# Two attention layers on one core: layer 1's sums of weights travel through DRAM instead of TensorE, and two kinds of steps change places

## The chip, the core and the metric

The kernel runs on one NeuronCore of a Trainium2 chip. Its engines run side by side and meet only through semaphores: TensorE (PE in the profile; PEld is its weight load), VectorE (DVE), ScalarE (ACT), GpSimd (POOL) and SyncE (SP), which here only issues DMAs. Each engine works off its own instructions in order. The metric is the device time of one execution in microseconds (us): 4741.2 us before the change, the median of three runs from 4740.61 to 4742.43.

## The reference, cut to what matters

The input has 2 images of 256 channels and 64 x 64 pixels, so 4096 positions each. Layer 0 is an attention over four heads of 16 channels with a gate; the change doesn't touch it. Layer 1, which the change is about, is this:

```python
qkv = jnp.einsum('oc,bchw->bohw', w_qkv, x) + b_qkv[None, :, None, None]
qkv = qkv.reshape(b, HEADS, 3 * head_dim, h * w)          # 4 heads of 64
q, k, v = jnp.split(qkv, 3, axis=2)
attn = jax.nn.softmax(jnp.einsum('bhdn,bhdm->bhnm', q, k) * scale, axis=-1)
out = jnp.einsum('bhnm,bhdm->bhnd', attn, v).reshape(b, c, h, w)
return jnp.einsum('oc,bchw->bohw', w_out, out) + b_out[None, :, None, None] + x
```

Note the reshape: the attention's output has the positions ahead of the head's channels, so it is read as channels only after it went through DRAM (the arrays `att`). Everything is float32.

## The kernel before, in words

**Tiling of layer 1.** A unit is `(b, g, j)`: one image, one pair of heads, one block of 512 queries; there are 32 units, worked off one after the other. A unit's 4096 keys come in 32 chunks of 128. A *step* of the loop at the end of the function handles two chunks, so a unit has 16 steps, and I count the steps of a unit from 0. The partitions of a score tile are 128 keys; its 1024 columns are 512 queries for each of the two heads.

**Work of one chunk.** PE multiplies keys with queries (`score`, L861). DVE takes the running maximum over the chunks (`keep`, L878), then ACT copies the scores to a tile `raw` in SBUF (L879). Ten steps later (`LAG`) DVE subtracts the maximum (`shift`, L944), ACT takes the exponential (`weigh`, L956), POOL adds the weights to an accumulator (L966 for the first two chunks of a group, L968 for all others), and PE multiplies the weights with the values (`gather`, L978). The tiles `raw` are a ring of 24.

**Groups.** A unit's chunks form two groups of 16. After the last chunk of each group the maximum is turned by PE (L886), folded by DVE (L898), split by POOL into three bfloat16 parts (`split`, L909 to L912), and turned back by PE (`turn`, L925): for group 0 in steps 8 and 9 of the unit, for group 1 in steps 0 and 1 of the next. ACT copies the row (L930), PE spreads it (L939), and only then can `shift` begin on that group. Because of the lag, the weights of group 0 are made from step 10 on, those of group 1 from step 2 of the next unit on. When a group's values are complete, ACT copies the result out of PSUM into a tile `avs` (L995), of which the pool has two buffers: for group 0 in step 2 of the next unit, for group 1 in its step 10.

**End of a unit,** in steps of the next unit: `total` (step 12) sums the accumulators over the 128 keys by PE into rows; `keep_total` copies them to SBUF (L1016); `turn_total` (step 13) turns the rows by four PE transposes (L1023), so that each query is on its own partition; `factors` joins both groups' sums and takes the reciprocal on DVE (L1035, L1036, L1038), and POOL makes the factor for group 0 (L1039). `turn_sums` turns each group's result (L1023), and `rows` multiplies it with the factor on DVE (L1049); POOL adds a bias (L1056) and joins the groups (L1060). In step 13 this is done for group 1, in step 14 for group 0. Then the rows go to `att` in DRAM.

**Work ahead.** The queries of the next unit are made in steps 14 and 15 (`next_queries`, L672; copied by ACT, L699). While units remain that have no keys and values yet (the first 24 units), each unit makes one block of them in steps 4 to 7. The output of image 0 is projected in four of the later units (`project_out`). One PSUM bank, `misc`, serves all of these small products in turn.

**What sets the order.** `at(t, place, step)` hangs a function onto a step at a named place: "start" and "early" come after the two score products, "early end" after the first chunk's `keep` and `shift`, "late" and "late end" after the second chunk's `keep` and after `gather`. Compute instructions keep this written order on every engine; DMAs are placed by the scheduler and wait, in order, on their queue. At the end `FILL` spreads first halves of the last output's projection over what is left.

Of the kernel before, what the change touches and what calls it, by code (L numbers as in the profile page):

```python
# [8 lines left out]
F32 = mybir.dt.float32  # L9
BF16 = mybir.dt.bfloat16  # L10
AF = mybir.ActivationFunctionType
ALU = mybir.AluOpType
# [3 lines left out]
P = 128  # L16
NB = 512
# [4 lines left out]
D1 = 64  # L22
# [5 lines left out]
def conv_attention_kernel(  # L28
# [739 lines left out]

    units = [(b, g, j) for b in range(B) for g in range(PR) for j in range(NJ)]
# [8 lines left out]
    with (  # L778
# [22 lines left out]
        )  # L801
        last_att = []
# [210 lines left out]
        def keep_total(u):  # L1013
            b, g, j = u
            row = l1.tile([P, NB], F32, tag="srow", bufs=1, name=f"srow_{b}_{g}_{j}")
            seq(nc.scalar.copy(row, srows[u]))  # L1016
            srows[u] = row
            seq(nc.scalar.activation(losts[u], losts[u], AF.Exp, scale=D1**-0.5))

        def turned(a, name):  # L1020
            ps = misc(name)
            for i in range(PB):
                seq(nc.tensor.transpose(ps[:, bass.ts(i, P)], a[:, bass.ts(i, P)], ident))  # L1023
            return ps.rearrange("p (i k d) -> p i k d", k=2, d=D1)

        def turn_total(u):
            srows[u] = turned(srows[u], "sumt_{}_{}_{}".format(*u))

        def factors(u):

            b, g, j = u
            ps = srows.pop(u)
            lost = losts.pop(u).rearrange("p k i -> p i k")
# [11 lines left out]
        def rows(u, n):  # L1045
            b, g, j = u
            ps = avs1.pop((u, n))
            r = l1.tile([P, PB, 2, D1], F32, tag="rows", name=f"rows_{b}_{g}_{j}_{n}")
            seq(nc.vector.tensor_tensor(  # L1049
                r, ps, joined[u][:, n].unsqueeze(3).to_broadcast([P, PB, 2, D1]), ALU.mult  # L1050
            ))
            last = u == units[-1]
            if n == 1:
                halves[u] = r
                bias = b1v[:, 2 * g : 2 * g + 2, :].unsqueeze(1).to_broadcast([P, PB, 2, D1])
# [53 lines left out]
        for n, u in enumerate(units):  # L1109
            b, g, j = u  # L1110
            t0 = n * US
            if n > 0:
                at(t0 - 5, "start", lambda u=u, b=b, j=j: fetch(("q", u), x1[b][j]))
                at(t0 - 2, "late", lambda u=u: next_queries(u, 0))
                at(t0 - 1, "early", lambda u=u: next_queries(u, 1))
                at(t0 - 1, "early end", lambda u=u: keep_queries(u))
# [24 lines left out]
            at(t1 + 5, "early", lambda u=u: turn_total(u))  # L1141
            at(t1 + 5, "early end", lambda u=u: factors(u))
            at(t1 + 5, "late", lambda u=u: turn_sums(u, 1))
            at(t1 + 5, "late end", lambda u=u: rows(u, 1))
            at(t1 + 6, "early", lambda u=u: turn_sums(u, 0))
            at(t1 + 6, "early end", lambda u=u: rows(u, 0))
            if b < B - 1 and (g, j) == (PR - 1, NJ - 1):
                for i in range(NJ):
                    t1 = t0 + US + (i + 4) * GS // 2
                    at(t1, "start", lambda b=b, i=i: fetch_output(b, i))  # L1150
                    for o in range(CC):
                        at(
                            t1 + 3 + 4 * o, ("early", "late")[o],
                            lambda b=b, i=i, o=o: project_out(b, i, o, misc(f"o1_{b}_{i}_{o}")),
                        )
                        at(t1 + 3 + 4 * o, "late end", lambda b=b, i=i, o=o: output(b, i, o))
# [51 lines left out]
        for i in range(NJ - 2):  # L1208
# [7 lines left out]
            (END + GS // 2 + 4, "early end"): (3,), (END + GS // 2 + 5, "early end"): (4,),  # L1216
            (END + GS // 2 + 5, "late end"): (5,), (END + GS // 2 + 6, "early end"): (6, 7),
# [87 lines left out]
```

## Time and profile before

| what | value |
|---|---|
| median of three runs | 4741.2 us |
| the profiled execution | 4741.58 us, of which 4739.8 us are the profile's span |
| layer 1's loop | about 2060 us to 4700 us of the span |
| one unit that makes keys and values | 81.30 us from its first L879 to the next unit's |
| one unit that makes none (the last 8) | 79.19 us |
| one of the four units with output | 88.75 us (the first of them 90.01 us) |
| PE, DVE, ACT, POOL busy in 2692.30 to 2773.60 us, one unit of 81.30 us | 76.70, 76.34, 68.51, 75.48 us |

The profile is of one execution; it gives, for every engine, the start and duration of each instruction and, where an engine was idle before it, whose semaphore ended the idle time. A row of a timeline has the start in us, the duration in us, engine, line and operation, output and inputs, and in brackets the idle time before it with its releaser. A row of the table of stages has a stretch and then the busy time of each engine in it. "SPq" is SyncE's DMA queue: the row tells when a DMA was issued, not when its data had landed.

### The profile page before, as it was taken

Reading aid. Unit: us, or ns where it says so; the run is one execution under the profiler, and the core shown is the slowest. Engines: PE = TensorE matmul, PEld = TensorE weight load, DVE = VectorE, ACT = ScalarE, POOL = GpSimd, SP = SyncE. Lnnn points to the kernel's source line nnn. Section 1 sums busy time; section 2 is a strip of 40 time slices with the busy share of each in tenths; the row PEclk is TensorE's granted clock in tenths of the full one; section 3 lists DMA queues with packets and bytes.
Section 4 is the critical chain, followed back from the end, with each engine's and each line's share of the span. In section 5 each row is a group of like instructions: output and inputs, shape, how many; then the busy total and the mean of one; then the engine's idle time right before and its main releaser. Section 6 shows DMA issues by size and latency. Waiting matters only on the chain.

```text
span 4739.8 us, 70643 instructions
## 1 busy us (share of the span) xinstructions
PE 4526.9 (96%) x27506; PEld 1496.2 (32%) x27506; DVE 3917.0 (83%) x4584; ACT 3394.1 (72%) x4508; POOL 2540.6 (54%) x1491
## 2 busy tenths in 40 slices
PE   8999999999999999989999999999999999999998
PEld 3433333333333333333232232323233332222222
DVE  6777777777777777359999999999999899999996
ACT  3366666666666666668888888888887778888884
POOL 6300000000000000039999999999998889999994
PEclk9999999999999999999999999999999999999999
DMA  3100000000000000110000100001111111000002
GB/s 103 34 4 19 19 21 15 15 15 15 15 15 15 15 13 13 57 63 25 23 25 17 54 30 23 25 23 36 52 36 45 63 52 47 18 14 7 14 16 74
DMA packets 113381, 140.10 MB, mean 30 GB/s; under 512 B 51864, under 2 KB 52696, under 8 KB 112932
## 3 DMA queue, kind: packets, MB, share of 16 engines
q1 hardware_dynamic: 111260, 135.11, 9.2%
q8 instruction: 216, 3.54, 0.3%
q14 instruction: 121, 0.99, 0.1%
q10 hardware_dynamic: 1784, 0.46, 0.0%
HBM read 93.58 MB, written 41.70 MB: 29 GB/s over the span
## 4 chain that ended last, share of the span: by engine, by line
PE 58%; DVE 15%; POOL 15%; issue 6%; ACT 5%; DMA 1%; SPq 0%; ACTq 0%; DVEq 0%; POOLq 0%
PE s L448 24%; POOL acc L968 13%; PE av L463 12%; DVE rmax L878 10%; PE s L861 6%; PE av L978 5%; DVE raw L944 4%; ACT raw L879 4%; PE a L410 2%; PE p L270 1%; PE k1p L672 1%; POOL acc L966 1%; PE rt L886 1%; PE q1p L672 1%; PE o L549 1%
## 5 line engine op out<-in xcount | busy, mean ns | idle before, releaser
L968 POOL TENSOR_TENSOR acc<-acc,raw 128x1024 f32<-128x1024 f32 x884 | 2098.1, 2373 | 89.4 <-ACT raw L956 30.2
L414 DVE TENSOR_REDUCE mx<-a 128x1 f32<-128x512 f32 x2048 | 1315.3, 686 | 450.5 <-PE a L410 449.4
L451 ACT ACTIVATE p<-s 128x512 f32<-128x512 f32 x2048 | 1109.8, 597 | 701.3 <-PE a L410 367.3
L944 DVE TENSOR_TENSOR raw<-raw,shift 128x1024 f32<-128x1024 f32 x1024 | 1238.0, 1213 | 19.2 <-PE shift L939 12.7
L861 PE MATMUL s<-q,k 64*128 64x512 f32 x4096 | 1117.2, 636 | 142.9 <-ACT raw L879 134.6
L878 DVE TENSOR_TENSOR rmax<-s,rmax 128x1024 f32<-128x1024 f32 x960 | 1170.1, 1219 | 72.7 <-PE s L861 70.8
L879 ACT COPY raw<-s 128x1024 f32<-128x1024 f32 x1024 | 1037.7, 1013 | 259.4 <-DVE rmax L878 173.5
L448 PE MATMUL s<-q,kT 32*128 32x512 f32 x4096 | 1219.1, 640 | 0.0
L956 ACT ACTIVATE raw<-raw 128x1024 f32<-128x1024 f32 x1024 | 1086.9, 1062 | 178.4 <-DVE raw L944 147.3
L410 PE MATMUL a<-kT,q 32*128 32x512 f32 x4096 | 1129.7, 643 | 1.2 <-DVE mx L414 1.0
L978 PE MATMUL av<-raw,v 128*64 128x512 f32 x4096 | 999.3, 606 | 2.0
L463 PE MATMUL av<-p,v 128*32 128x256 f32 (+1 forms) x7904 | 650.2, 399 | 0.6 <-ACT avs L477 0.6
L861 PEld LDWEIGHTS s<-q,k 64*128 64x128 f32 x4096 | 317.1, 185 | 827.9 <-ACT raw L879 628.0
L513 POOL TENSOR_TENSOR f<-f,dyn 128x16 f32<-128x16 f32 x15 | 3.3, 223 | 1028.2 <-DVE f L512 1028.2
L448 PEld LDWEIGHTS s<-q,kT 32*128 32x128 f32 x4096 | 397.9, 183 | 426.3 <-issue 392.1
L978 PEld LDWEIGHTS av<-raw,v 128*64 128x64 f32 x4096 | 243.3, 136 | 587.6 <-issue 428.8
L463 PEld LDWEIGHTS av<-p,v 128*32 128x32 f32 x7904 | 157.6, 108 | 751.5 <-issue 737.3
L564 POOL TENSOR_SCALAR res<-res 128x1024 f32<-128x1024 f32 x16 | 16.8, 1049 | 660.5 <-ACT res L563 660.5
L410 PEld LDWEIGHTS a<-kT,q 32*128 32x128 f32 x4096 | 305.0, 184 | 31.4 <-DVE mx L414 18.2
L966 POOL TENSOR_TENSOR acc<-raw,raw 128x1024 f32<-128x1024 f32 x64 | 152.4, 2381 | 112.7 <-ACT raw L956 103.8
L898 DVE TENSOR_REDUCE negs<-rt 128x4 f32<-128x512 f32 x128 | 88.3, 690 | 50.1 <-PE rt L886 47.6
L318 DVE RECIPROCAL std<-std 128x128 f32<-128x128 f32 x64 | 56.1, 920 | 37.7 <-ACT std L313 37.7
(332 smaller groups left out, 1840.4 us busy)
## 6 DMA issues: line engine op xcount, KB each, us to landing
x<-in_x_dram SPq DMA_DIRECT2D x16, 512.0 KB
res<-in_x_dram SPq DMA_DIRECT2D x16, 512.0 KB
x<-res SPq DMA_DIRECT2D x16, 512.0 KB
att<-rows SPq DMA_DIRECT2D x62, 128.0 KB
kd<-k1s SPq DMA_DIRECT2D x24, 256.0 KB
vd<-v1s SPq DMA_DIRECT2D x24, 256.0 KB
k<-kd SPq DMA_DIRECT2D x24, 256.0 KB
v<-vd SPq DMA_DIRECT2D x24, 256.0 KB
```

What stands on the lines that cost most here:

```text
L410: seq(nc.tensor.matmul(ps, qs0[u][r, bass.ts(i, P)], kTs[b][r, bass.ts(m, NB)], start=True, stop=True,))
L414: seq(nc.vector.tensor_reduce(mxs[u][:, i * H + h, m : m + 1], ps, AX.X, ALU.max))
L448: seq(nc.tensor.matmul(ps, kTs[b][r, bass.ts(m, P)], qs0[u][r, :], start=True, stop=True))
L451: seq(nc.scalar.activation(pt[:, k, :], ps, AF.Exp, scale=D0**-0.5))
L463: seq(nc.tensor.matmul(avs[u][32 * h : 32 * h + 32, cols], vs0[b][:, m, 32 * h : 32 * h + 32], pts[t, h // 2][:, h % 2, cols], start=(m == ...
L861: seq(nc.tensor.matmul(ps[:, k, :], ks[b, g, m // PB][r, bass.ts(m % PB, P)], qs1[u][r, :], start=True, stop=True,))
L878: seq(nc.vector.tensor_tensor(rmax[u, n], ps, before, ALU.max))
L879: seq(nc.scalar.copy(raw, ps))
L944: seq(nc.vector.tensor_tensor(raws[t], raws[t], shifts[u, t % NM // GS], ALU.add))
L956: seq(nc.scalar.activation(p, p, AF.Exp, scale=D1**-0.5))
L968: seq(nc.gpsimd.tensor_tensor(accs[u, n], accs[u, n], p, ALU.add))
L978: seq(nc.tensor.matmul(avs1[u, n][k * D1 : (k + 1) * D1, :], v[:, m % PB, k, :], raws[t][:, k, :], start=(m % GS == 0), stop=(m % GS == GS ...
```

## The change

Four things change.

- **The sums of weights.** The four PE transposes of `turn_total` and the two DVE operations at the start of `factors` are gone. `keep_total` writes the rows in a permuted order, four DMAs send one row each to DRAM, and one DMA reads them back so that each query's sums are on its partition, 1024 pieces of two floats. A new `add_sums`, at the late end of step 13, joins the groups by two GpSimd operations of 128 x 8. All five DMAs are on SyncE's queue.
- **The rows.** `factors` moves to the start of step 15; both `turn_sums` and both `rows` move to step 3 of the unit after that, one "early", one "late". Group 0 of the unit in between asks for its `avs` tile in step 2 of that same unit, one step ahead. The order of the two small inner dimensions of `rows` changes with it.
- **The queries** of the next unit are made "early" in steps 13 and 14 instead of "late" in 14 and "early" in 15, and fetched one step sooner.
- **The output and the end.** The projections of image 0 are hung onto other steps, all "late". The last unit's rows no longer go to the tile `last_att` by eight DMAs from SBUF, but to `att` in DRAM and from there to the tile, one store and one load on each of two queues. `FILL` is adapted.

```diff
@@ layer 1, set-up
+        sum1 = {
+            u: dram.tile([NG * 2, NB], F32, tag="sum_{}_{}_{}".format(*u), name=f"sum_{u}")
+            for u in units
+        }
@@ keep_total
-            seq(nc.scalar.copy(row, srows[u]))
-            srows[u] = row
+            seq(nc.scalar.copy(
+                row.rearrange("p (a m i) -> p a i m", m=P, i=2),
+                srows[u].rearrange("p (a i m) -> p a i m", m=P, i=2),
+            ))
+            for m in range(2 * NG):
+                nc.sync.dma_start(out=sum1[u][m : m + 1, :], in_=row[32 * m : 32 * m + 1, :])
+            s = small.tile([P, NG, 2, PB], F32, tag="sums1", name=f"sums1_{b}_{g}_{j}")
+            nc.sync.dma_start(
+                out=s.rearrange("p n k (a i) -> p (n k a) i", i=2),
+                in_=sum1[u].rearrange("m (a p i) -> p (m a) i", p=P, i=2),
+            )
+            srows[u] = s
@@ turn_total becomes add_sums
-        def turn_total(u):
-            srows[u] = turned(srows[u], "sumt_{}_{}_{}".format(*u))
+        def add_sums(u):
+            s, lost = srows[u], losts[u]
+            seq(nc.gpsimd.tensor_tensor(s[:, 0], s[:, 0], lost, ALU.mult))
+            seq(nc.gpsimd.tensor_tensor(s[:, 1], s[:, 1], s[:, 0], ALU.add))
@@ factors
-            s = small.tile([P, PB, 2], F32, tag="sum1", name=f"sum1_{b}_{g}_{j}")
-            seq(nc.vector.tensor_tensor(s, ps[:, :, 0, ::32], lost, ALU.mult))
-            seq(nc.vector.tensor_tensor(s, s, ps[:, :, 1, ::32], ALU.add))
-            f = small.tile([P, NG, PB, 2], F32, tag="f1", name=f"f1_{b}_{g}_{j}")
-            seq(nc.vector.reciprocal(f[:, 1], s))
-            seq(nc.gpsimd.tensor_tensor(f[:, 0], f[:, 1], lost, ALU.mult))
+            f = small.tile([P, NG, 2, PB], F32, tag="f1", name=f"f1_{b}_{g}_{j}")
+            seq(nc.vector.reciprocal(f[:, 1], srows.pop(u)[:, 1]))
+            seq(nc.gpsimd.tensor_tensor(f[:, 0], f[:, 1], losts.pop(u), ALU.mult))
@@ rows, the last unit
-            if last:
-                for k in range(2):
-                    c = ((2 * g + k) * N + j * NB) // D1 % P
-                    for i in range(PB):
-                        (nc.sync if k else nc.scalar).dma_start(
-                            out=last_att[0][c + 2 * i : c + 2 * i + 2, :].rearrange(
-                                "q (s d) -> q s d", d=D1
-                            ),
-                            in_=r[:, i, k, :],
-                        )
-                return
...
-                nc.sync.dma_start(
+                queue = (nc.sync, nc.scalar)[k if last else 0]
+                queue.dma_start(
                     out=to[2 * g + k, bass.ts(j, NB), :].rearrange("(i q) d -> q i d", q=P),
-                    in_=r[:, :, k, :],
+                    in_=r[:, k, :, :],
                 )
+                if last:
+                    c = ((2 * g + k) * N + j * NB) // D1
+                    queue.dma_start(
+                        out=last_att[0][c % P : c % P + NB // D1, :],
+                        in_=att[b][c : c + NB // D1, :],
+                    )
@@ the steps
-                at(t0 - 5, "start", lambda u=u, b=b, j=j: fetch(("q", u), x1[b][j]))
-                at(t0 - 2, "late", lambda u=u: next_queries(u, 0))
-                at(t0 - 1, "early", lambda u=u: next_queries(u, 1))
-                at(t0 - 1, "early end", lambda u=u: keep_queries(u))
+                at(t0 - 6, "start", lambda u=u, b=b, j=j: fetch(("q", u), x1[b][j]))
+                for c in range(CC):
+                    at(t0 - 3 + c, "early", lambda u=u, c=c: next_queries(u, c))
+                at(t0 - 2, "early end", lambda u=u: keep_queries(u))
...
-            at(t1 + 5, "early", lambda u=u: turn_total(u))
-            at(t1 + 5, "early end", lambda u=u: factors(u))
-            at(t1 + 5, "late", lambda u=u: turn_sums(u, 1))
-            at(t1 + 5, "late end", lambda u=u: rows(u, 1))
-            at(t1 + 6, "early", lambda u=u: turn_sums(u, 0))
-            at(t1 + 6, "early end", lambda u=u: rows(u, 0))
+            at(t1 + 5, "late end", lambda u=u: add_sums(u))
+            at(t1 + 7, "start", lambda u=u: factors(u))
+            for place, k in (("early", 1), ("late", 0)):
+                at(t1 + 11, place, lambda u=u, k=k: turn_sums(u, k))
+                at(t1 + 11, f"{place} end", lambda u=u, k=k: rows(u, k))
...
-                    for o in range(CC):
+                    for o, step in enumerate((t1 + 3 - i % 2, t1 + 7)):
                         at(
-                            t1 + 3 + 4 * o, ("early", "late")[o],
+                            step, "late",
...
-            (END + GS // 2 + 4, "early end"): (3,), (END + GS // 2 + 5, "early end"): (4,),
-            (END + GS // 2 + 5, "late end"): (5,), (END + GS // 2 + 6, "early end"): (6, 7),
+            (END + GS // 2 + 4, "early end"): (3, 4), (END + GS // 2 + 11, "early end"): (5,),
+            (END + GS // 2 + 11, "late end"): (6, 7),
```

More of the change, by code (lines that the diff above doesn't have):

```diff
@@ L1023, in turned @@
                 seq(nc.tensor.transpose(ps[:, bass.ts(i, P)], a[:, bass.ts(i, P)], ident))
[L1024 to L1027 removed]
+            return ps.rearrange("p (i k d) -> p k i d", k=2, d=D1)
+        def add_sums(u):
+            s, lost = srows[u], losts[u]
+            seq(nc.gpsimd.tensor_tensor(s[:, 0], s[:, 0], lost, ALU.mult))
+            seq(nc.gpsimd.tensor_tensor(s[:, 1], s[:, 1], s[:, 0], ALU.add))
         def factors(u):
             b, g, j = u
[L1032 to L1039 removed]
+            f = small.tile([P, NG, 2, PB], F32, tag="f1", name=f"f1_{b}_{g}_{j}")
+            seq(nc.vector.reciprocal(f[:, 1], srows.pop(u)[:, 1]))
+            seq(nc.gpsimd.tensor_tensor(f[:, 0], f[:, 1], losts.pop(u), ALU.mult))
             joined[u] = f
@@ L1047, in rows @@
             ps = avs1.pop((u, n))
-            r = l1.tile([P, PB, 2, D1], F32, tag="rows", name=f"rows_{b}_{g}_{j}_{n}")
+            r = l1.tile([P, 2, PB, D1], F32, tag="rows", name=f"rows_{b}_{g}_{j}_{n}")
             seq(nc.vector.tensor_tensor(
-                r, ps, joined[u][:, n].unsqueeze(3).to_broadcast([P, PB, 2, D1]), ALU.mult
+                r, ps, joined[u][:, n].unsqueeze(3).to_broadcast([P, 2, PB, D1]), ALU.mult
             ))
@@ L1054, in rows @@
                 halves[u] = r
-                bias = b1v[:, 2 * g : 2 * g + 2, :].unsqueeze(1).to_broadcast([P, PB, 2, D1])
+                bias = b1v[:, 2 * g : 2 * g + 2, :].unsqueeze(2).to_broadcast([P, 2, PB, D1])
                 seq(nc.gpsimd.tensor_tensor(r, r, bias, ALU.add))
@@ L1150, in conv_attention_kernel @@
                     at(t1, "start", lambda b=b, i=i: fetch_output(b, i))
-                    for o in range(CC):
+                    for o, step in enumerate((t1 + 3 - i % 2, t1 + 7)):
                         at(
-                            t1 + 3 + 4 * o, ("early", "late")[o],
+                            step, "late",
                             lambda b=b, i=i, o=o: project_out(b, i, o, misc(f"o1_{b}_{i}_{o}")),
                         )
-                        at(t1 + 3 + 4 * o, "late end", lambda b=b, i=i, o=o: output(b, i, o))
+                        at(step, "late end", lambda b=b, i=i, o=o: output(b, i, o))
         last_x, first_half = [], []
```

## The prediction

> **What bounds the kernel now.** I read the page from the top (busy shares, the slices, the groups), then the table of stages for two units, the waits of layer 1, and timelines around every step that the change touches. From the page:
>
> ```profile
> span 4739.8 us, 70643 instructions
> ...
> PE 4526.9 (96%) x27506; PEld 1496.2 (32%) x27506; DVE 3917.0 (83%) x4584; ACT 3394.1 (72%) x4508; POOL 2540.6 (54%) x1491
> ...
> DVE  6777777777777777359999999999999899999996
> ...
> POOL 6300000000000000039999999999998889999994
> ...
> L968 POOL TENSOR_TENSOR acc<-acc,raw 128x1024 f32<-128x1024 f32 x884 | 2098.1, 2373 | 89.4 <-ACT raw L956 30.2
> ```
>
> PE's 96% is of the whole span. In layer 1 (slices 18 to 40) DVE and POOL are as full. Two units, one that makes keys and values and one of the last eight, in the table of stages:
>
> ```profile
> 2692.30:2773.60 81.30, 76.70 (x330) 24.33 (x328) 76.34 (x73) 68.51 (x74) 75.48 (x43) 1.00 0.15 46
> 4260.80:4339.97 79.17, 72.82 (x310) 21.64 (x308) 76.06 (x72) 67.86 (x73) 75.40 (x43) 1.00 0.04 11
> ```
>
> Three engines are within 1 us of each other in the first; with some 0.07 us of issue behind each operation, POOL's 31 additions (2.45 us apart) and small ones make 77.9 of 81.3 us. So each step has its own limit. DVE's four operations hold any step to 4.52 us; steps longer than that wait for PE. Where does POOL matter? Waits from 2200 to 4600 us:
>
> ```profile
> ACT raw L879 <- DVE rmax L878: 151.4, 275, 1.1
> ...
> POOL acc L966 <- ACT raw L956: 87.7, 59, 2.5
> ...
> PEld L925 <- POOL negmax L912: 50.3, 33, 2.0
> ```
>
> POOL stops before L966, the first addition of a group (steps 3 and 11), and between two of these runs through. What slack it has is there: from step 3 to 11 it works 37.8 of 40.28 us (38.17 in the last eight units), from step 11 to step 3 40.15 of 41.02. And PE waits for POOL's `split` once a unit. The timelines of steps 2 and 3, and of step 9 in one of the last eight units:
>
> ```profile
> 2787.26 1.01 ACT L879 COPY raw<-s 128x1024 f32<-128x1024 f32 x1 [0.15 <-DVE rmax L878]
> 2788.18 0.59 ACT L995 COPY avs<-av 128x512 f32<-128x512 f32 x1
> ...
> 2788.33 1.13 PE L861 MATMUL s<-q,k 64*128 64x512 f32 x4 [0.65 <-ACT raw L879]
> 2788.65 1.07 ACT L956 ACTIVATE raw<-raw 128x1024 f32<-128x1024 f32 x1
> ...
> 2789.80 2.38 POOL L966 TENSOR_TENSOR acc<-raw,raw 128x1024 f32<-128x1024 f32 x1 [0.87 <-ACT raw L956]
> ```
>
> ```profile
> 4307.10 0.24 POOL L912 TENSOR_TENSOR negmax<-rest,negmax 128x8 bf16<-128x8 f32 x1
> ...
> 4307.40 0.40 PE L925 MATMUL nm1p<-ident,negmax 128*128 128x128 bf16 x4 [1.07 <-POOL negmax L912]
> ```
>
> **What the Trainium skill says.** "Perfetto Trace Analysis", Optimization Strategy: the same gap repeating on an engine can mean that there is no room for the next tile, by buffer count or size. The 59 equal waits at L966 aren't of that kind (the trace names the exponential), but the change makes one: `avs` has two buffers. "DMA: Bandwidth & Descriptors", Anatomy of one DMA: about 2.0 us fixed, mostly until the write is confirmed (stated for DMAs issued by GpSimd). Layer 0 sends its sums the same way, on SyncE's queue:
>
> ```profile
> 917.96 1.12 SPq L502 DMA_DIRECT2D sum<-avs  x4
> ...
> 920.00 0.35 SPq L506 DMA_DIRECT2D f<-sum  x1
> ```
>
> The load is issued when the stores have landed (919.98), 2.02 us after the first was issued; it lands at 921.74, after 1.74 us. This agrees. The same page, Rules for kernel authors: a last dimension that isn't contiguous becomes one descriptor per element. That fits the new load's 1024 pieces of 8 bytes; no run of before shows so many.
>
> **The change part by part** (us per unit).
>
> *Steps 12 to 0.* Four PE transposes leave (0.66), eight of `turned` (1.31), DVE's two sums (0.16 each), a reciprocal that now runs at a step's start, and two `rows` (0.6 each with issue). Both query halves (1.06 each) stay but come earlier, where PE has the transposes' place. Steps 12 to 15 last 5.2, 5.7, 5.2 and 4.5, step 0 6.5: above 4.52, so PE sets them. Step 13 has a query half in place of eight transposes, -0.26; step 14 loses four, -0.66; step 15 is at DVE's 4.5 already and wins nothing from its 1.06; step 0 wins some 0.3, because its scores no longer wait for queries just made (26 waits of L861 for ACT's L699, 0.9 each). Sum **-1.2**; a walk through the timeline agrees (step 0's fold at 2773.4 instead of 2774.59). Bounds -0.8 and -2.4 (the latter if step 1, where POOL holds PE up by 0.5, also gains).
>
> *The `avs` buffer.* ACT's L995 in step 2 now needs a buffer which `turned` of the unit before frees only in step 3. The copy stood at 2788.18. PE's new `turned(1)` follows the second score product of step 3's early part, 2788.33 to 2789.46, plus 0.66: 2790.12. The copy so starts at 2790.15, **1.97 late**, and behind it in ACT's order stand the exponential of 2788.65 and the copy of scores of 2789.61; POOL's L966 (0.87 of waiting, for just that exponential) goes 1.9 later. DVE, which also gets both `rows` here (4.52 + 2 x 0.6 against a step of 4.4), moves 2.4. In steps 4 to 7 PE sets the pace in units with keys and values (4.8 to 5.3 per step), and of this +1.75 is left; in the last eight these steps are at 4.5, DVE's own, and nothing is won back. The bounds are 0 (all hidden in ACT's 19% of idle time) and 2.5.
>
> *Rows on POOL.* Two additions of 1.24, 2.48 in all, leave the stretch from step 11 to 3 (slack 0.87) and enter that from 3 to 11: 37.8 + 2.48 = 40.28, just the 40.28 that it lasts. With L966 1.9 late, `split` of group 0 comes 4.4 late in step 9. PE had 1.06 of margin there in units with keys and values, and the delay of steps 3 to 7 gives it 1.75 more: 4.4 - 1.06 - 1.75 = 1.6, of which 0.85 stays after what step 10 (5.0 against 4.52) and 9 can absorb: **+0.85**. The last eight have no margin (PE waits 1.07 already): +2.48 there on top of 1.9. `add_sums` adds 0.46 in the other stretch, which has won 2.48.
>
> *The sums through DRAM.* In the unit shown the row would be out of ACT at 2755.62. Stores landed about 2757.8 (2.02 plus issue), the load 1.7 plus 64 - 8 pieces per DMA engine. The page gives no price for a piece of 8 bytes; layer 0's 64-byte pieces take 25 to 50 ns, so 56 x 0.03 = 1.6: landed at 2761.1. POOL comes to `add_sums` at 2763.4. **Nothing**, hidden behind POOL's additions of steps 12 and 13, with 2.3 to spare. The upper bound is 0.145 us a piece, from the parameters' 8-byte loads at the start (8 in 1.16 us): 9.3 us, POOL stops 4.6. The same queue carries key and value loads; they stand there blocked for at most these few us and are due steps later, as are the query fetches, one step sooner. ACT's permuted L1016 (0.59 now) is costed as before; ACT is idle 19% of the time, and were it twice as long, 0.6 of that goes.
>
> *Output and end.* Four output units: three small products now share step 3 with the one `misc` bank, +1.5 more. At the end the last store and load go behind x's loads on SyncE (free about 4709; sums loaded about 4712, rows stored 4718.5, loaded 4721.3) against 4718.78 when PE goes on now: **+2.5**.
>
> Sum: 18 units with keys and values, -1.2 + 1.75 + 0.85 = +1.4: 25.2. Eight last, -1.2 + 1.9 + 2.48 = +3.2: 25.6. Four with output +2.9: 11.6. The second unit, with nothing ahead of it, -1.2. End +2.7. Together +64 on the profiled 4741.6 (its own span 4739.8; 0.4 above the median, so nothing to correct): 4805. Walks by hand leave out small slacks, so I take 4799.
>
> **The rivals.**
> *A, slower by buffer and POOL* as above: 4765 to 4835. For it: the `avs` order is fixed by the program, and L912 and L966 are already the places where someone waits for POOL. Chance 0.55.
> *B, the sums come late.* Above 0.075 us a piece (4.2 for 56, against 1.6 + 2.3 of cover) POOL waits in step 13. At 0.145 it stops 4.6, of which 3.5 remain after POOL's 0.87 and the 2.48 that left: 31 x 3.5 = +108, which partly covers A's costs (who is late anyway loses no more at step 3): 4815 to 4900. Against it: layer 0's 1.74. Chance 0.16.
> *C, absorbed.* ACT is idle 19%, POOL 0.87 at step 3, PE 0.65; the late copy eats these and only the last eight pay, 8 x 3.2 + 2.7 = 28 less 23 x 0.6, makes 4756, range 4732 to 4765. Chance 0.16.
> *D, faster.* POOL's stretch from 11 to 3 is the tighter one (40.15 of 41.02), and 2.48 leave it. If `split` of group 1 in step 1 comes earlier, the unit wins 2.4 there, and the 2.5 into steps 3 to 11 fit (37.8 + 2.48 = 40.28). It decides if the `avs` wait costs below 1.2: 30 x -1.2 = -36: 4705, range 4690 to 4731. Against it: 1.97 of wait on an engine whose next two instructions are both waited for. Chance 0.13.
>
> **How the numbers follow.** 0.2% of 4741, 9.5 us, is about what a measurement tells from no change. D gives faster 0.13; half of C lies within 0.2%, same 0.08; A, B and the rest of C slower, 0.79. The likeliest is A, 4799, its own range 4765 to 4835; with C's upper part and B's lower, 4735 to 4855 hold 8 in 10.
>
> **What would show it.** L995 idle before it with PE's `turned` as releaser, near 2 us, once a unit; L966's wait growing past 2 us; L925's wait for L912 going from 33 times to about 60; the units' periods at about 82.7, 91.6 and 82.4; the stretch from step 12 to 1 shorter by 1.2; no wait of POOL's `add_sums` for a DMA. B would show as just that wait, some 4 us. I am wrong if step 3 isn't longer, or if 12 to 0 win over 2.

## The result, and the profile after

The changed kernel takes 4795.1 us (median of four runs, 4791.15 to 4795.35) against 4741.6 us: a ratio of 1.0111, 95% interval 1.0094 to 1.0129. It is slower by 1.1%. The forecast was 4799 us.

The page of the changed kernel, from its top. Lines of the program after L800 are moved by five to fifteen: L884 is the old L879, L961 the old L956, L971 and L973 the old L966 and L968, L1000 the old L995.

```profile
span 4793.3 us, 70549 instructions
...
PE 4514.3 (94%) x27378; PEld 1480.7 (31%) x27378; DVE 3906.7 (82%) x4520; ACT 3392.7 (71%) x4508; POOL 2548.3 (53%) x1555
...
DVE  6777777777777777279999999999988899899996
...
L973 POOL TENSOR_TENSOR acc<-acc,raw 128x1024 f32<-128x1024 f32 x884 | 2096.8, 2372 | 77.3 <-ACT raw L961 20.6
```

TensorE is busy for 13 us less than before, DVE for 10 us less and GpSimd for 8 us more, and the span is 53.5 us longer: what the kernel lost is nearly all waiting. The waits of layer 1 (2200 to 4650 us) say where. Columns: who waited for whom, us in total, times, longest.

```profile
POOL acc L971 <- ACT raw L961: 133.6, 59, 4.2
ACT raw L884 <- DVE rmax L883: 132.0, 263, 1.8
...
PEld L930 <- POOL negmax L917: 91.2, 49, 3.9
...
ACT avs L1000 <- PE turned L1038: 54.2, 30, 1.8
...
PE nm1p L930 <- POOL negmax L917: 48.7, 25, 3.0
```

The fourth row is new: the copy into `avs` waits once per unit, 1.8 us each time, for TensorE to turn the previous unit's tile. GpSimd's wait at the first addition of a group is 133.6 us where it was 87.7, and the weight load's wait for the split 91.2 where it was 50.3. The timeline of steps 2 and 3 of a unit with keys and values shows the first link, the one whose counterpart in the prediction started at 2788.18 without a wait:

```profile
2709.22 1.13 PE L866 MATMUL s<-q,k 64*128 64x512 f32 x4 [0.64 <-ACT raw L884]
...
2710.28 0.66 PE L1038 MATMUL turned<-ident,avs 128*128 128x128 f32 x4
2710.97 0.58 ACT L1000 COPY avs<-av 128x512 f32<-128x512 f32 x1 [1.81 <-PE turned L1038]
...
2711.45 1.06 ACT L961 ACTIVATE raw<-raw 128x1024 f32<-128x1024 f32 x1
```

ACT stands still for 1.81 us until the transposes, which stand behind a score product, are done; the exponential behind it is the one that GpSimd's first addition waits for. The second link, in step 9 of one of the last eight units:

```profile
4340.55 0.23 POOL L917 TENSOR_TENSOR negmax<-rest,negmax 128x8 bf16<-128x8 f32 x1
...
4340.84 0.40 PE L930 MATMUL nm1p<-ident,negmax 128*128 128x128 bf16 x4 [2.98 <-POOL negmax L917]
```

TensorE waited 1.07 us here before, now 2.98. Two units in the table of stages (stretch, length, then busy time of PE, PEld, DVE, ACT, POOL with the number of instructions; the next figure is the mean clock granted to TensorE, 1.00 being all of it):

```profile
2694.69:2776.67 81.98, 75.94 (x326) 23.82 (x324) 76.04 (x71) 68.51 (x75) 75.47 (x45) 1.00 0.15 43
4290.04:4372.02 81.98, 72.27 (x306) 21.12 (x304) 75.75 (x71) 67.95 (x72) 75.71 (x45) 1.00 0.05 10
```

Both kinds of unit have the same length now, though the second has 3.7 us less to do on TensorE: in the second, TensorE's own work doesn't set the length. The first two of the last eight units are longer still, 84.41 and 83.57 us. The second of them and the unit behind it, as wholes and in step 9:

```profile
4124.50:4208.07 83.57, 73.92 (x306) 21.68 (x304) 75.86 (x71) 67.96 (x72) 75.41 (x45) 0.98 0.04 10
4208.07:4290.04 81.97, 72.31 (x306) 21.14 (x304) 75.76 (x71) 67.97 (x72) 75.73 (x45) 1.00 0.04 10
```

```profile
4175.28 0.40 PE L930 MATMUL nm1p<-ident,negmax 128*128 128x128 bf16 x4 [2.96 <-POOL negmax L917]
4175.61 3.66 PE L866 MATMUL s<-q,k 64*128 64x512 f32 x8
...
4258.85 0.40 PE L930 MATMUL nm1p<-ident,negmax 128*128 128x128 bf16 x4 [2.96 <-POOL negmax L917]
4259.17 1.99 PE L866 MATMUL s<-q,k 64*128 64x512 f32 x8
```

Behind the same wait the same eight products take 3.66 us in one unit and 1.99 in the next: from 4175.6 us on, the trace grants TensorE half of its clock for 3.41 us. Between the first unit and the last copy of scores, the 13 profiles of this case have 59 such stretches of half clock, the kernel before none. Each comes with a wait for the split that lasted 1.67 us or more; no shorter wait has one, and 26 of the 85 longer ones have none either. The traces show what makes the difference. In each run all these stretches start at whole multiples of 3.413 us from each other, so I cut the loop into windows of that length. All 59 follow a window in which TensorE was busy for 1.67 us or less, and of the 9643 windows that aren't followed by one, only four were as little busy. So a wait for the split can cost more than its length, when enough of it falls into one window. No run tested this alone. In the changed kernel only these two units have half clock, some 4 us in all; in several of the experiments many units have it, and there it matters.

Cut into stretches of steps (from the first copy of scores of one step to that of the next, means over units 3 to 17 and 23, and over 25 to 30, counted from 0), in us:

| | steps 0-2 | 3-7 | 8-11 | 12-15 | unit |
|---|---|---|---|---|---|
| keys and values, before | 15.98 | 24.74 | 19.98 | 20.61 | 81.31 |
| after | 17.71 | 24.59 | 20.35 | 19.34 | 81.99 |
| last eight, before | 15.98 | 22.52 | 20.07 | 20.65 | 79.22 |
| after | 17.71 | 23.05 | 22.15 | 19.32 | 82.24 |

The last row contains the unit with half clock; without it steps 8 to 11 are 21.89 and the unit 81.98. A copy that is late in step 2 lengthens the column 0-2. Steps 12 to 15 did win, 1.3 us; steps 2, 3 and 9 gave it back and more.

The round trip through DRAM, which was the change's main point, is hidden. SyncE's queue and GpSimd in steps 12 and 13:

```profile
2759.38 0.64 ACT L1021 COPY srow<-sum 128x512 f32<-128x512 f32 x1
2760.04 1.12 SPq L1026 DMA_DIRECT2D sum_(0, 0, 7)_19303<-srow  x4
...
2762.20 0.39 SPq L1028 DMA_DIRECT2D sums<-sum_(0, 0, 7)_19303  x1
2767.70 0.20 POOL L1043 TENSOR_TENSOR sums<-sums,lost 128x8 f32<-128x8 f32 x1
```

The trace records the landing at 2764.36, 2.16 us after the load's issue and 3.34 us before L1043, which has no wait. Over the 31 units inside the loop the margin is 0.8 to 3.5 us, mostly 3.3.

At the end of the kernel it is not hidden:

```profile
4742.79 0.62 ACT L1021 COPY srow<-late_sums 128x512 f32<-128x512 f32 x1 [1.25 <-PE late_sums L1013]
...
4744.44 1.15 SPq L1026 DMA_DIRECT2D sum_(1, 1, 7)_19327<-srow  x4
4757.09 0.38 SPq L1028 DMA_DIRECT2D sums<-sum_(1, 1, 7)_19327  x1
4759.33 0.20 POOL L1043 TENSOR_TENSOR sums<-sums,lost 128x8 f32<-128x8 f32 x1 [20.78 <-DMA sums<-sum_(1, 1, 7)_19327]
...
4766.36 0.53 ACTq L1084 DMA_DIRECT2D last_att<-att  x1
...
4772.48 3.31 PE L1202 MATMUL o<-last_att,wo 128*128 128x512 f32 x4 [4.93 <-DMA last_att<-att]
```

The four stores, 8 KB in all, count as landed only 12.65 us after their issue; 1792 KB of `last_att` and 1024 KB of x had been issued just ahead of them, and the trace has packets of these loads until 4756.3 us. From the last copy of scores to the end of the span it is 96.1 us, before 85.2.

### The profile page after: what moved, and what is told of

It is laid out like the page before. It is cut to its first block, busy times and chain, and to the rows that moved or that the text cites. A ratio compares the mean times of both kernels' runs of the same rounds, so it can differ in the third digit from the quotient of the medians.

```text
span 4793.3 us, 70549 instructions
## 1 busy us (share of the span) xinstructions
PE 4514.3 (94%) x27378; PEld 1480.7 (31%) x27378; DVE 3906.7 (82%) x4520; ACT 3392.7 (71%) x4508; POOL 2548.3 (53%) x1555
## 4 chain that ended last, share of the span: by engine, by line
PE 64%; DVE 16%; POOL 7%; issue 7%; ACT 5%; DMA 1%; SPq 0%; ACTq 0%; POOLq 0%; DVEq 0%
PE s L448 24%; PE av L463 12%; DVE rmax L883 11%; PE s L866 9%; PE av L983 8%; POOL acc L973 6%; DVE raw L949 4%; ACT raw L884 4%; PE a L410 2%; PE q1p L672 1%; PE p L270 1%; PE k1p L672 1%; PE rt L891 1%; PE v1p L705 1%; PE o L549 1%
## 5 line engine op out<-in xcount | busy, mean ns | idle before, releaser
L973 POOL TENSOR_TENSOR acc<-acc,raw 128x1024 f32<-128x1024 f32 x884 | 2096.8, 2372 | 77.3 <-ACT raw L961 20.6
L961 ACT ACTIVATE raw<-raw 128x1024 f32<-128x1024 f32 x1024 | 1085.5, 1060 | 189.7 <-DVE raw L949 156.0
L884 ACT COPY raw<-s 128x1024 f32<-128x1024 f32 x1024 | 1035.6, 1011 | 232.1 <-DVE rmax L883 154.4
L971 POOL TENSOR_TENSOR acc<-raw,raw 128x1024 f32<-128x1024 f32 x64 | 151.8, 2372 | 160.5 <-ACT raw L961 151.5
L891 PE MATMUL rt<-ident,rmax 128*128 128x128 f32 x512 | 84.0, 287 | 3.1 <-DVE negs L903 2.6
```

The costliest lines, as they stand in the source:

```text
L884: seq(nc.scalar.copy(raw, ps))
L961: seq(nc.scalar.activation(p, p, AF.Exp, scale=D1**-0.5))
L973: seq(nc.gpsimd.tensor_tensor(accs[u, n], accs[u, n], p, ALU.add))
```

## The experiments

All start from the changed kernel unless another is named; ratios are to the kernel before, with the 95% interval. I had two theories for the loop, which can both hold: **the buffer** (ACT waits for `avs`, and the exponentials behind it) and **GpSimd's load** (the row additions delay the split in step 9), and against both the plain rival that the work moved into step 3 costs what it costs there. For the sums, that the round trip is hidden, or is not.

### A third buffer

```diff
-a = l1.tile([P, NB], F32, tag="avs", name=...)
+a = l1.tile([P, NB], F32, tag="avs", bufs=3, name=...)
-row = l1.tile([P, NB], F32, tag="srow", bufs=1, name=...)
+row = l1.tile([P, NB], F32, tag="rows", name=...)
```

> Theory, the buffer: with a third buffer ACT's copy into avs in step 2 waits for nothing; PE's eight transposes, DVE's two row products and POOL's two additions stay in step 3. Units with keys and values go from 81.98 to 81.1 to 81.5 us, the last eight from 81.98 to 80.2 to 80.6, the end wins about 3: 4755 to 4775 in all, estimate 4764, against 4795. Rival, the work itself: if step 3 is late because of the work moved there and not because of the buffer, the wait goes and the time stays at 4788 to 4796. (The row of sums shares its two buffers with the rows, to make room; no wait is expected of that.)

Measured: 4757.9 us, 1.0033 (1.0020 to 1.0046). ACT's wait is gone:

```profile
2700.74 0.59 ACT L1000 COPY avs<-av 128x512 f32<-128x512 f32 x1
2701.22 1.07 ACT L961 ACTIVATE raw<-raw 128x1024 f32<-128x1024 f32 x1
...
2702.37 2.39 POOL L971 TENSOR_TENSOR acc<-raw,raw 128x1024 f32<-128x1024 f32 x1 [1.42 <-ACT raw L961]
```

The buffer alone was worth 37 us, about 70% of the loss. Steps 0 to 2 fall from 17.71 to 15.82 us; steps 3 to 7 rise from 24.59 to 25.66, so a part of the wait had covered the work moved there, as the rival has it, but no more than a part. Two sizes were off. Units with keys and values come to 80.6, half a us better than I expected, because most of the wait for the split goes too (steps 8 to 11: 19.85). Of the last eight, two come to 80.1, as expected or a little better; five are at 81.3 to 81.7, and these five have a stretch of half clock in step 9, behind a wait for the split that is still 1.9 us long: there GpSimd's load is in the way. The end didn't win the 3 us that I expected (97.0 us).

### GpSimd's additions behind the split

The product of the rows stays in step 3; the bias and the join go to a function of their own.

```diff
             for place, k in (("early", 1), ("late", 0)):
                 at(t1 + 11, place, lambda u=u, k=k: turn_sums(u, k))
                 at(t1 + 11, f"{place} end", lambda u=u, k=k: rows(u, k))
+                if u not in units[-2:]:
+                    at(t1 + 17, "start", lambda u=u, k=k: join(u, k))
```

> POOL's two row additions move from step 3 to the start of step 9, just behind the split. Theory, POOL late at the split: TensorE's waits for the split (139.9 us by the table of waits in layer 1) fall to about those of before (71.6) or less; units with keys and values win 0.4, the last eight 2.1: 4768 to 4778 in all. Rival, the late exponential alone makes the split late: 4790 to 4796.

Measured: 4767.7 us, 1.0056 (1.0041 to 1.0071).

```profile
ACT avs L1000 <- PE turned L1038: 54.2, 30, 1.8
...
PEld L930 <- POOL negmax L917: 44.6, 36, 2.2
...
PE nm1p L930 <- POOL negmax L917: 13.3, 15, 1.4
```

The buffer's wait is as it was, the split's is below that of before. Steps 8 to 11 are back at 19.8 and 20.0 us. So the split was late because of GpSimd's 2.48 us in step 3, and this was worth 27 us, most of it in the last units (80.3 us instead of 82 and more; with the long wait, the half clock is gone as well, 4 of the 27 us).

### Both, and the end as before

First the end alone: the last unit's sums by TensorE, its rows by eight DMAs to the tile.

```diff
+if u == units[-1]:
+    at(t1 + 5, "early", lambda u=u: old_total(u))
+    at(t1 + 5, "early end", lambda u=u: old_factors(u))
...
+if last:
+    for k in range(2):
+        c = ((2 * g + k) * N + j * NB) // D1 % P
+        for i in range(PB):
+            (nc.sync if k else nc.scalar).dma_start(
+                out=last_att[0][c + 2 * i : c + 2 * i + 2, :].rearrange(
+                    "q (s d) -> q s d", d=D1
+                ),
+                in_=r[:, k, i, :],
+            )
+    return
```

> Only the last unit's sums go by TensorE, and its rows by eight DMAs straight to the last tile, as in the kernel before. Theory, the trip through DRAM at the end costs the 29.1 less 22.3 us that lie between the row of sums and the last projection: 4788.5, range 4786 to 4791. Rival, the new order of the end's work costs it: 4793 to 4797.

Measured: 4788.6 us, 1.0097 (1.0082 to 1.0112). The end shrinks from 96.1 to 90.9 us, the loop is the same to 0.7 us. Then the three edits in one kernel:

> Third buffer, POOL's additions in step 9 and the end as in the kernel before, all three. Theory, these are separate costs and add up: units with keys and values 80.6 us, the last eight 79.3 to 79.6, those with output 89.9, the end as long as before or 2 us longer: 4734, range 4728 to 4742. Rival, they cover each other (who waits at the buffer does not wait at the split): not below 4745.

Measured: 4734.9 us, 0.9986 (0.9979 to 0.9993), with 80.6, 79.4 and 89.5 to 90.7 us for the three kinds of unit. The rival is refuted, but the costs don't simply add up: one by one the three edits gained 37, 27 and 6.5 us, 71 in sum, and together they gain 60, so a part of them was covered by another (the third buffer alone had removed most of the wait for the split in units with keys and values). With the three gone, what is left of the change is a gain, if one of 0.14%.

### The sums by TensorE

```diff
-at(t1 + 5, "late end", lambda u=u: add_sums(u))
-at(t1 + 7, "start", lambda u=u: factors(u))
+at(t1 + 7, "early", lambda u=u: old_total(u))
+at(t1 + 7, "early end", lambda u=u: old_factors(u))
```

> The sums go by TensorE again (four transposes, two DVE operations of 0.16 us), in step 15, where the bank is free; rows and queries stay as changed. Theory, the round trip is hidden: TensorE gets 0.66 and DVE 0.3 us more per unit, the end wins the 4 to 7 us of its round trip: 4795 to 4812, estimate 4802. Rival, the round trip costs time in the loop: below 4785.

Measured: 4812.1 us, 1.0149 (1.0132 to 1.0166). Without the round trip the loop is longer, by 0.55 us in units with keys and values (step 15: 4.30 to 4.76) and by some 1.8 on average in the last; the end is 88.8, 7.3 us shorter. The trip by itself is a good part of the change, except for the last unit, against transposes in step 15. The last units lost more than I allowed for because six of these seven have half clock in step 9 (83.6 to 85.2 us); the one that hasn't lasts 82.53, 0.55 more than in the changed kernel, as the others do.

### The queries back

```diff
-for c in range(CC):
-    at(t0 - 3 + c, "early", lambda u=u, c=c: next_queries(u, c))
-at(t0 - 2, "early end", lambda u=u: keep_queries(u))
+at(t0 - 2, "late", lambda u=u: next_queries(u, 0))
+at(t0 - 1, "early", lambda u=u: next_queries(u, 1))
+at(t0 - 1, "early end", lambda u=u: keep_queries(u))
```

> Only the queries go back to steps 14 late and 15 early. Step 13 then wins 0.45 (TensorE loses 1.06, DVE holds the step at 4.52), step 15 loses 0.6, step 0 waits for queries just made, 0.2 to 0.3: 0.4 per unit worse, 4807 in all, range 4800 to 4816. Rival, the gain of steps 12 to 0 is all due to the transposes that left: 4791 to 4798.

Measured: 4815.4 us, 1.0157 (1.0142 to 1.0172). In units with keys and values it went as expected: step 13 is 4.52 instead of 4.97, step 0 6.45 instead of 6.28, the unit 82.3, and the wait for queries just made is there again:

```profile
PEld s L866 <- ACT q L699: 31.7, 26, 1.2
```

But step 14 grew by 0.43 and step 15 by 0.15 only, where I expected 0.6 in step 15; and the last units rose to between 83.4 and 84.7, where I expected 0.4 more than 82.0. The trace says why: all of them have half clock in step 9, behind the same wait of 2.96 us as in the changed kernel, where two have it. Their other steps are longer by 0.3 us, as in units with keys and values.

### The sums needed earlier

```diff
-at(t1 + 5, "late end", lambda u=u: add_sums(u))
+at(t1 + 4 if u != units[-1] else t1 + 5, "late end", lambda u=u: add_sums(u))
```

> POOL joins the sums one step earlier, two additions or 4.9 us; they land 3.3 us before they are needed now, so POOL waits some 1.6 us in each unit but the last. Theory, POOL has this to spare between step 11 and step 3 since the rows left it: within 0.2%, 4788 to 4801. Rival, POOL's waits for the sums cost their time: 31 x 1.6, 4845.

Measured: 4830.2 us, 1.0185 (1.0168 to 1.0202). My theory was wrong here. GpSimd waits 1.70 us in the median unit, 1.93 on average, and in units with keys and values the wait arrives at TensorE in step 1 of the next unit whole (1.86 us on average at both places; medians 1.61 and 1.63). Most of these units are 82.4 to 82.7 us long, 0.5 more than in the changed kernel; the four with half clock in step 1 are 84.2 to 86.6, and all of the last eight have it in step 1 or 9. So of the 35 us lost some 20 come with the half clock (an estimate: what these units last above those without, less the 4 us of the changed kernel). One of the longer waits that is not followed by half clock:

```profile
2604.65 0.20 POOL L1043 TENSOR_TENSOR sums<-sums,lost 128x8 f32<-128x8 f32 x1 [2.15 <-DMA sums<-sum_(0, 0, 5)_19301]
...
2625.48 0.23 POOL L917 TENSOR_TENSOR negmax<-rest,negmax 128x8 bf16<-128x8 f32 x1
...
2625.76 0.40 PE L930 MATMUL nm1p<-ident,negmax 128*128 128x128 bf16 x4 [2.19 <-POOL negmax L917]
```

In the changed kernel TensorE doesn't wait at this place in step 1 at all, before the change it waited 0.56 in most units with keys and values. The account: the rows took 2.48 us from GpSimd there and `add_sums` added 0.46, so 2.02 were freed; 0.56 of these ended TensorE's wait, and 1.44 were used up because steps 12 to 0 became that much shorter. Next to nothing is left over, and so GpSimd's wait reaches TensorE. The next run tests this account without a DMA in play.

### GpSimd's additions in step 13

```diff
+                if u not in units[-2:]:
+                    at(t1 + 21, "late end", lambda u=u, k=k: join(u, k))
```

> POOL's two row additions, 2.48 us, go to the end of step 13 (they were in steps 13 and 14 before the change, and in step 9 in the run that moved them behind the split); all else as changed. Theory, what the rows and the shorter steps took from POOL ahead of the split in step 1 are about equal, so TensorE waits there for POOL by 2.3 more: 81.47 + 2.3 = 83.8 us in units with keys and values, 4832 in all, range 4815 to 4845. Rival, the loss of the run with earlier sums came from its waits for DMAs and not from POOL's time: 4768, as with the additions in step 9.

Measured: 4836.7 us, 1.0200 (1.0186 to 1.0214), units with keys and values at 83.5 to 85.1, the mean 84.4. The split in step 9 is no longer late, that in step 1 is:

```profile
PEld L930 <- POOL negmax L917: 106.9, 45, 3.5
PE nm1p L930 <- POOL negmax L917: 65.6, 34, 2.6
```

TensorE's wait is near what the theory says, 2.58 us in most units for 2.3. The same 2.48 us in 30 units cost 69 us more in step 13 than in step 9, 2.3 per unit. About half of this comes with the half clock, and the theory, which left that out, hit its number by luck: all units with keys and values that have the wait have half clock in step 1. Three of the last eight (25, 26 and 30, counted from 0) haven't and last 81.6 us, against 80.3 with the additions in step 9: there the place alone costs 1.3 us. One of these three and the unit behind it:

```profile
4246.21:4327.79 81.58, 72.31 (x306) 21.13 (x304) 75.88 (x71) 67.94 (x72) 75.79 (x45) 1.00 0.04 11
4327.79:4411.54 83.75, 75.19 (x306) 21.99 (x304) 76.06 (x71) 67.94 (x73) 75.78 (x45) 0.96 0.04 10
```

So the gain of steps 12 to 0 needs the rows to be gone from there: the row move that did the harm is also what paid for the rest.

### Another order of the groups

With two buffers, the tile of group 0 has to be turned before step 2 and that of group 1 before step 10. So take group 0 first.

```diff
-for place, k in (("early", 1), ("late", 0)):
-    at(t1 + 11, place, lambda u=u, k=k: turn_sums(u, k))
-    at(t1 + 11, f"{place} end", lambda u=u, k=k: rows(u, k))
+plan = ((0, (7, "late"), (8, "start"), (10, "late end")),
+        (1, (18, "early"), (20, "start"), (20, "late end")))
```

The three places of a group are those of its transposes, its product and its addition on GpSimd, in steps after `t1`. Group 0 gets the bias, group 1 the join; the last two units keep step `t1 + 11` for group 1 (the last for both).

> Two buffers as in the changed kernel, but group 0 of the rows first: turned late in step 15, multiplied at the start of step 0, its bias added by POOL late in step 2 ahead of the first addition of the group, where POOL waits anyway; group 1 turned early in step 10, multiplied at the start of step 12, joined at its end. No turned tile is late for a buffer. The end is as in the kernel before; two output products move to steps 12 and 14. Theory (buffer, POOL and the full engines of step 3 are all of the cost): units with keys and values 80.1 to 80.5 us, the last eight 78.4 to 78.8, 4718 in all, range 4708 to 4735. Rival, the steps that take the work stretch by it: 4740 or more.

Measured: 4747.5 us, 1.0013 (1.0006 to 1.0019). No `avs` wait, yet the rival was right: 81.2 and 79.1 us for the two kinds of unit. Steps 10 and 11 are 0.7 and 0.6 us longer than with the three edits, and DVE waits for TensorE's `shift` (L944) 60 times:

```profile
DVE raw L949 <- PE shift L944: 34.0, 60, 1.0
```

I had put the transposes of step 10 ahead of the `shift` product that DVE was waiting for; 36 such waits cost 10.9 us in the changed kernel. The second place then was chosen where TensorE has nothing urgent behind it:

```diff
-        (1, (18, "early"), (20, "start"), (20, "late end")))
+        (1, (11, "late"), (11, "late end"), (17, "start")))
-for o, step in enumerate((t1 + 3 + i % 2, t1 + 7 - i % 2)):
+for o, step in enumerate((t1 + 2, t1 + 7 - i % 2)):
```

> As the run with the other order (group 0 turned late in step 15, multiplied at the start of step 0, its bias late in step 2), but group 1 turned and multiplied late in step 3 and joined by POOL at the start of step 9. Theory: the run with the other order lost 1.2 us in steps 10 and 11 and 0.6 in 13 by what it put into steps 10 and 12; without that, and with one group instead of two in step 3, units with keys and values last 79.7 to 80.2 us, the last eight 78.9 to 79.4: 4716 in all, range 4705 to 4728. Rival, half of the work costs as much in step 3 as all of it: 4735 or more.

Measured: 4723.2 us, 0.9961 (0.9947 to 0.9974): faster than both kernels. A unit with keys and values and one of the last eight:

```profile
2682.67:2762.64 79.97, 75.69 (x326) 23.82 (x324) 76.06 (x71) 68.45 (x74) 75.54 (x45) 1.00 0.15 44
4237.57:4316.16 78.59, 72.26 (x306) 21.12 (x304) 75.84 (x71) 67.80 (x72) 75.77 (x45) 1.00 0.05 11
```

The busy times are those of the changed kernel to 0.3 us; 2.0 and 3.4 us of waiting are gone. No unit has half clock. Units with output hardly won (89.9 for 90.4; 88.75 before the change): their products, moved to other steps here, lengthen steps 2 and 14.

### The rest of the end

```diff
 if u == units[-1]:
-    plan = ((1, (11, "early"), (11, "early end"), (11, "early end")),
-            (0, (11, "late"), (11, "late end"), (11, "late end")))
+    plan = ((1, (5, "late"), (5, "late end"), (5, "late end")),
+            (0, (6, "early"), (6, "early end"), (6, "early end")))
+elif u == units[-2]:
+    plan = ((0, (7, "late"), (7, "late end"), (7, "late end")),
+            (1, (8, "early"), (8, "early end"), (8, "early end")))
```

`FILL` is the one of the kernel before.

> The best of the runs so far (group 0 first, 4723.2) lasts 93.6 us from the last copy of scores to the end of the span, the kernel before 85.2. Here the rows of the last unit but one are made right at the end of the loop instead of three steps behind it, and the last unit's rows and the spread of the half projections are as in the kernel before. Theory, the rows hung behind the loop cost the end its other part (the trip through DRAM was the first): 86 to 88 us, 4716 in all, range 4712 to 4720. Rival, the end is longer for another reason: 4721 or more.

Measured: 4720.6 us, 0.9956 (0.9943 to 0.9970), the end at 91.0 us. Between the theory and the rival: every part of the end from the row of group 1's maximum on is back to the length of before within 0.15 us, except that the last transfer is 1.4 shorter; but the part ahead of it, from the last copy of scores to that row, is 20.2 instead of 13.2 us. The rows put at the loop's end now stand in it, and TensorE has half clock there for 6.83 us from 4631.4 on, which the kernel before hasn't; which of the two costs how much wasn't tested, nor was a better place for the rows looked for.

## Why the prediction was right, and which sizes were off

The direction, the two mechanisms and, nearly, the time (4799 for 4795.1) are borne out. The sum is less well matched than its total. It came to 64 us, or 4805; the 6 us taken off for "small slacks" weren't worked out. By its own terms (us of span, measured as differences of unit lengths between the two profiles):

| term | forecast | measured |
|---|---|---|
| 18 units with keys and values | +25.2 | +12.5 |
| last eight units | +25.6 | +25.6 |
| four units with output | +11.6 | +6.5 |
| second unit | -1.2 | -1.5 |
| start of the loop and first unit | 0 | -0.4 |
| end | +2.7 | +10.9 |
| sum | +64 | +53.5 |

- **Steps 12 to 0.** Forecast -1.2; measured -1.44 (1.27 in steps 12 to 15, 0.17 in step 0). Right, though not step by step: step 13 won 0.74 for 0.26 forecast, step 14 0.38 for 0.66. Taking the queries back returns step 0's part and the wait for queries. Not seen in advance was that this gain is worth just what GpSimd was relieved of (the runs with earlier sums and with additions in step 13).
- **The buffer.** The copy was to be 1.97 late and was 1.81. Forecast +1.75 in units with keys and values after what steps 4 to 7 win back; measured 1.90 in step 2, 0.54 in step 3, -0.69 in steps 4 to 7: 1.75. In the last eight nothing is won back, as said: +2.44. The sum has 1.9 there, though by its own reasoning (DVE moves 2.4, nothing won back) it should have had 2.4. The third buffer, worth 37 of the 53.5 us, shows it to be the largest cost.
- **Rows on GpSimd.** Forecast +0.85 and +2.48; measured in steps 8 to 11 +0.37, and +1.82 in the last eight where the clock is whole. The first is the term that was mis-sized most often, 18 times: step 10 took back 0.35 of the 0.80 that step 9 lost, and I had counted less. The additions behind the split, alone, remove both.
- **The last eight units.** That their total is met to a tenth is luck: 2.8 us per unit where 3.2 was forecast, and some 4 us from the half clock in two of them, which the prediction didn't have.
- **Sums through DRAM.** "Nothing" was right, the margin larger (3.3 for 2.3): the load took 2.16 us and not 3.3. The trace has 1024 packets of 8 bytes for it, one for each pair of floats, so the rule on single elements that the prediction names describes only a neighbouring case. Rival B, late sums, is refuted for this placement. Its price was mis-summed: 4.6 less 0.87 and 2.48 leaves 1.25, not 3.5. Where the sums are late by 1.7 to 1.9 us, the kernel lost 35 us against the changed one, a little over 1.1 per unit, more than half of it with the half clock.
- **Output units.** +1.5 of contention for the bank was too much: measured +1.6 in all, where +2.9 was said.
- **The end.** This is the term that failed: +10.9 where the text has 2.5 and the sum 2.7. The queueing of the stores behind the loads was sized well (the sums loaded 16.1 us after their row's copy began by forecast, 16.4 measured). The load of the last rows was not: 2.8 us by forecast (4718.5 to 4721.3), 6.1 from its last issue to the projection; why it takes so long stays open. And I left out that the last unit but one hangs its rows into the end as well: 1.6 us of buffer wait and 2.7 in front of group 1's tile. The end as before gives back 5.2 of the 10.9.

The errors of the end and of the units with keys and values cancel in part; the total is nearer than its terms deserve. Of the signs named in advance, the `avs` wait (30 times 1.8), the wait at the first addition (2.3 us each), the missing wait of `add_sums` and the shorter steps 12 to 0 came as said; step 1 is as long as before. The load's wait for the split went from 33 to 49 times and not 60, and the unit lengths were 82.0, 90.4 and 82.0 for 82.7, 91.6 and 82.4.

Rival D had one thing right: GpSimd's stretch from step 11 to step 3 was the tighter one and was relieved. But the gain of 2.4 us that it expected in step 1 isn't there, and with the buffer's wait gone the kernel was still slower than before (4757.9). A total in D's range (4690 to 4731) came only with group 0 first (4723.2 and 4720.6); the third buffer, the later additions and the old end together stay above it (4734.9).

## What to carry to other kernels

When a step moves past the point where its pool's next tile is asked for, the wait falls on whoever fills that tile and on everything queued behind it; here moving one of two groups ahead of that point undid it without a further buffer. The price of a small operation on a nearly full engine can depend on its place more than on its length: 2.48 us of GpSimd work cost 2.3 us per unit more ahead of the split than directly behind it, so look for the instruction that others wait for and put the work behind it. When a wait costs more than its length, look at the granted clock: of these 2.3 us, only 1.3 are there in units whose clock is whole. And cost the last iteration by itself: what is hidden in the loop lies open there, behind whatever large transfers were just issued.

## What the runs showed of the hardware

Reading back 1024 pieces of 8 bytes took 2.1 to 2.3 us in most units. Layer 0's load of 128 pieces of 64 bytes took 1.74 us where the prediction shows it, 1.65 in the median of its 15 loads. The pieces per DMA engine, if spread evenly over 16, are 64 and 8, so each further piece comes to about 7 to 9 ns by this estimate ((2.16 - 1.74) / 56 and (2.16 - 1.65) / 56), where 30 were estimated and 145 feared. Two of the 32 loads took longer, 3.54 and 4.16 us, and three about 2.7; why wasn't looked into. Four stores of 2 KB that follow 2816 KB of loads on the same queue were confirmed 12.65 us after issue, 0.8 us after the last packets of x, against about 2.2 us in the loop: their size says nothing of their time.

TensorE's clock is granted in steps of 3.413 us here: it was halved for one or two such steps behind a step in which TensorE had been busy for 1.67 us or less, and eight products then took 3.66 us for 1.99.
